# Branch hints and five unread products at the seam between layer 0's front and the joint stage

## The chip, the cores and the metric

The kernel runs on one core of a Trainium2 chip. The metric is the device time of one execution in microseconds (us), lower is better. The profile comes from one further execution of the same program, recorded by the hardware profiler. Names used below: PE is TensorE (PEld its weight loads), DVE is VectorE, ACT is ScalarE, POOL is GpSimd, SP is the engine that issues most transfers. A trailing q (DVEq) means the engine's sequencer: branches, register loads, semaphore work.

## What is computed

The reference is a network of two layers on an image of 64 x 64 pixels with 96 channels. Each layer is a mixer with a residual and then a small MLP with a residual:

```
x = x + conv_ref(ln(x))          # a state-space mixer
t = t + ffn_ref(ln(t))           # t: x as 4096 tokens
```

Layer 0's mixer projects to 192 channels and a gate, applies a 3 x 3 depthwise convolution and silu, and scans the 4096 positions in four directions with 16 states for each channel:

```
log_dA = dt * A;  dB_u = dt * B * u
decay = exp(cumsum(log_dA))
h = decay * cumsum(dB_u / (decay + 1e-12))
y = sum_n(h * C) + u * D_skip
```

The four results are added, normalized, gated and projected back. In layer 0 the decay is so strong that, for inputs like these, only the first positions of each scan direction contribute; the full scan is needed only if the decay is weak. Layer 1's mixer has a full 3 x 3 convolution over channels and a recurrent scan. The MLPs round their operands to 8-bit floats.

## The kernel before, in words

All data of one image stay in on-chip memory as far as possible; the 4096 positions are handled in chunks of 512. The program has these stages in time.

Layer 0's front (`front0`, which calls `scan_ends`) runs from the start to about 102 us. It normalizes, projects and convolves the image, and beside that computes the ends of the four scans, 160 positions each, on small tiles. The order of its instructions is written out: `keep` holds an instruction in program order. The last lines of `scan_ends` (L840 to L867) are, on DVE, the scans of the ends, their product with C and the sums over states (L849, L850); then the smallest decay exponent `low` (L852) and the flag `alive` (L854), which is 1 if the full scan is needed. On PE there are fourteen products of the identity with itself into a bank `warm` that nobody reads (L860), and then two products `yc` (L863) which bring the last part of the ends to both halves of the partitions. `values_load` (L864) loads the flag into a register of each engine. `add_ends` (L875) then adds the ends to the image `y` on DVE, sixteen operations.

The branch is in `layer0` (L317): `with tc.If(self.alive > 0)` holds the full scan `scan_all`. With these inputs the flag is 0, so every engine jumps over the body. In the built program the code of the body lies between the front and what follows (1262 instructions on DVE, 515 on PE, 1201 on ACT, 295 on SP, 221 on POOL). Each engine takes its own branch and, on the path that skips the body, sets semaphores to what the body would have left them at; the stage behind the branch waits for them.

The joint stage (`middle`, L1100 on) does the rest of layer 0 and the front of layer 1 together. It first allocates tiles and issues weight loads on SP and memsets on POOL (`open1`, L1251 to L1287), takes eight banks of PSUM (`slots("bank", ...)`), and issues ten products of the identity with itself into the first bank, which nobody reads (L1129 and L1130). Then a planner takes over: `Order` holds operations with costs, dependencies and leads (`LEAD`), and its `run` writes them out in a fixed order for each engine. The first planned work is `mix0`: means over channels on PE (L1363, L1367), their subtraction on DVE (L1371, L1375), squares on ACT (L1378), the gate on POOL (L1382), variances on PE (L1398).

From about 300 us to the end the scans of layer 1 run (L1998 on DVE, with ACT, POOL, PE and transfers beside), and last layer 1's MLP.

Of the kernel before, what the change touches and what calls it, by code (L numbers as in the profile page):

```python
# [39 lines left out]
P = 128  # L40
# [223 lines left out]
class Net:  # L264
# [37 lines left out]
    def layer0(self, w, w1):  # L302

        tc = self.tc
        self.pools0 = ctx = ExitStack()
        wp = ctx.enter_context(tc.tile_pool(name="mw0", bufs=1))
        yp = ctx.enter_context(tc.tile_pool(name="my0", bufs=1))
        pp = ctx.enter_context(tc.tile_pool(name="pad0", bufs=1))
        self.weights0(wp, w)
        self.y = [yp.tile([P, L // (1 + g)], F32, tag=f"y{g}", name=f"y0{g}") for g in range(2)]  # L310
        pad = self.padded0(pp)
        self.bc_d = [self.scratch(f"bc0{o}", [2, NST, L]) for o in range(2)]
        self.dt_d = [self.scratch(f"dt0{g}", [P, L]) for g in range(2)]
        self.du_d = [self.scratch(f"du0{g}", [P, L]) for g in range(2)]
        self.u_d = [self.scratch(f"u0{g}", [GP[g], L]) for g in range(2)]
        self.front0(wp, w, w1, pad)
        with tc.If(self.alive > 0):  # L317
            self.scan_all()

    def weights0(self, wp, w):  # L320
# [369 lines left out]
    def scan_ends(self, ep, pm, ps, pad, ue, beside):  # L690
# [4 lines left out]
        nc, keep = self.nc, self.keep  # L695
# [12 lines left out]
        o = 0  # L708
# [60 lines left out]
        for i, at in enumerate((XB, XC)):  # L769
            rows = self.dram.tile([4, TS], F32, tag=f"re{i}", name=f"re{i}")  # L770
            t = tile6(f"bce{i}", TS)
            o = 0
# [25 lines left out]
        buckets, o = [], 0  # L798
        for n0, n1, k in BUCKETS:
            buckets.append((n0, n1, n1 - n0, k, slice(o, o + (n1 - n0) * k)))  # L800
            o = buckets[-1][-1].stop
# [42 lines left out]
        for n0, n1, m, k, at in buckets[1:]:  # L844
            add = x[:, :, at]
            if m > 1:
                add = sums[:, :, 0:k]
                states = x[:, :, at].rearrange("p s (n t) -> p s t n", n=m)
                keep(nc.vector.tensor_reduce(add, states, AX.X, ALU.add))  # L849
            keep(nc.vector.tensor_tensor(x[:, :, 0:k], x[:, :, 0:k], add, ALU.add))  # L850
        low = ep.tile([1, 1], F32, tag="low", name="low")
        keep(nc.vector.tensor_reduce(low, t[0:1, 0:P], AX.X, ALU.min))  # L852
        alive = self.cp.tile([1, 1], I32, tag="alive", name="alive")
# [4 lines left out]
        warm = ps.tile([P, CH], F32, tag="e", name="warm")  # L858
# [2 lines left out]
        yc = [pm.tile([P, TE], F32, tag="m", name=f"yc{w}") for w in range(2)]  # L861
        for t, r in zip(yc, LANES):
            keep(nc.tensor.matmul(t, self.dup[r], x[r, 5], start=True, stop=True))  # L863
        self.alive = nc.values_load(  # L864
            alive, min_val=0, max_val=1, skip_runtime_bounds_check_because="the result of a comparison"
        )
# [230 lines left out]
    def keep(self, instruction):  # L1097
        self.tc.keep_in_program_order(instruction)

    def middle(self, w, pool):  # L1100
# [10 lines left out]
        nc, tc = self.nc, self.tc  # L1111
# [12 lines left out]
        def slots(tag, p, n, shape, dtype=F32):  # L1124
            o.slots(tag, [p.tile(shape, dtype, tag=f"{tag}{i}", name=f"{tag}{i}") for i in range(n)])

        pb = banks.enter_context(tc.tile_pool(name="ps_mid", bufs=1, space=PSUM))
        slots("bank", pb, 8, [P, CH])
        for _ in range(10):  # L1129
            self.keep(nc.tensor.matmul(o.free["bank"][0][1][:, 0:P], self.ident, self.ident, start=True, stop=True))  # L1130
        bp = back.enter_context(tc.tile_pool(name="back0", bufs=1))
        for tag, n, shape, dtype in (
            ("r", 2, [P, 2, 4], F32),
# [1443 lines left out]
```

## Time and profile before

| what | us |
|---|---|
| median of three runs (1229.6 to 1230.89) | 1230.8 |
| time of the profiled execution | 1231.9 |
| its span | 1229.9 |
| front's last DVE addition ends (L875) | 102.33 |
| ten unread products begin (L1130) | 105.00 |
| first mean begins (L1363) | 109.34 |
| first subtraction begins (L1371) | 113.22 |
| PE's mean granted clock over the span | 0.877 |

All times below the span are counted from the span's start. Busy time of an engine is time in its data path; waiting and sequencer work are not in it. A product in 32-bit floats takes two passes of PE, so ten products appear as twenty rows. The view of one line lists what ran on each engine and sequencer for that line, with the shortest, median and longest duration in ns and the first and last start. The view of narrow stretches gives busy times of PE, PEld, DVE, ACT and POOL, then the clock that PE was granted (1.00 is full speed), then how busy the transfers were.

### The profile page before, as it was taken

To read this page: it belongs to the slowest core of one execution; us is meant where nothing else is said; L and a number is where in the kernel's file an instruction comes from. 1 tells how busy PE (TensorE), PEld (TensorE's weight loads), DVE (VectorE), ACT (ScalarE), POOL (GpSimd) and SP (SyncE) were. 2 spreads that over 40 slices of the span, in tenths; PEclk is the share of its full clock that TensorE was granted. 3 is DMA by queue.
4 is the path that set the end of the run, shared out by engine and by line. 5 is a ranking of instruction groups with operands and counts; after the bars stand their busy time and mean duration, and the time that the engine had idled before them with its cause. 6 is when DMAs were issued, how large, how long until landed. Compare 5 with 4: busy or idle time off the path is not lost.

```text
span 1229.9 us, 11118 instructions
## 1 busy us (share of the span) xinstructions
PE 1013.7 (82%) x3498; PEld 414.7 (34%) x3498; DVE 1134.9 (92%) x908; ACT 881.8 (72%) x1065; POOL 842.4 (68%) x510
## 2 busy tenths in 40 slices
PE   9997889985278877887787877889778889888986
PEld 5533334321023322222332222233224444343344
DVE  7895787788898999999999999999999999999968
ACT  5682555656568878877888777878878878887626
POOL 3002364352678888888798878987798888886756
PEclk9998989995589887889978788988789999988987
DMA  2252010476763573575734585545736766432201
GB/s 76 67 174 53 1 27 20 124 245 193 235 193 126 182 237 125 172 230 172 239 112 127 194 258 166 180 146 185 233 115 194 246 195 235 142 101 83 103 1 52
DMA packets 79132, 183.14 MB, mean 149 GB/s; under 512 B 21534, under 2 KB 34936, under 8 KB 77688
## 3 DMA queue, kind: packets, MB, share of 16 engines
q1 hardware_dynamic: 78376, 182.16, 47.6%
q8 instruction: 29, 0.48, 0.2%
q14 instruction: 39, 0.32, 0.1%
q10 hardware_dynamic: 688, 0.19, 0.1%
HBM read 159.73 MB, written 21.52 MB: 147 GB/s over the span
## 4 chain that ended last, share of the span: by engine, by line
DVE 46%; issue 11%; PE 10%; ACT 5%; DMA 2%; POOL 1%; SPq 0%; another core or an unknown queue 0%; DVEq 0%; POOLq 0%; ACTq 0%
DVE h1s L1998 14%; DVE xws L1998 13%; DVE h0s L1998 8%; PE hs L2009 4%; DVE x2s L1998 3%; DVE x0s L1998 3%; DVE x1s L1998 3%; PE hs L2013 2%; ACT da L1983 2%; ACT xws L1968 2%; DMA x2s<-bc 1%; PE eo L2123 1%; PE da L2326 1%; POOL hss L2003 1%; DMA kept<-xn 1%
## 5 line engine op out<-in xcount | busy, mean ns | idle before, releaser
L2026 POOL TENSOR_TENSOR kept<-kept,kept 128x1024 f32<-128x1024 f32 x92 | 216.7, 2356 | 82.3 <-issue 40.2
L2003 POOL TENSOR_TENSOR hss<-h1s,xws 128x1024 f32<-128x1024 f32 x96 | 228.0, 2377 | 55.2 <-DVE xws L1998 52.4
L2009 PE MATMUL hs<-h0s,ident 128*128 128x512 f32 x360 | 222.9, 705 | 27.6 <-DVE h0s L1998 24.0
L1983 ACT ACTIVATE da<-dt1s,a 128x1024 f32<-128x1024 f32 x168 | 187.5, 1117 | 71.3 <-DVE xws L1998 55.3
L1998 DVE TENSOR_TENSOR_SCAN xws<-da,xws 128x1024 f32<-128x1024 f32 x96 | 221.6, 2308 | 10.4 <-ACT da L1983 10.3
L1983 ACT ACTIVATE da<-dt0s,a 128x1024 f32<-128x1024 f32 x166 | 185.1, 1115 | 45.1 <-DVE h0s L1998 16.2
L2013 PE MATMUL hs<-hss,ident 128*128 128x512 f32 x368 | 188.1, 603 | 15.4 <-POOL hss L2003 15.3
L1998 DVE TENSOR_TENSOR_SCAN h1s<-da,h1s,xws 128x1024 f32<-128x1024 f32 x72 | 167.3, 2323 | 0.3
L2037 PE MATMUL acc<-kept,fold 128*32 128x512 f32 x368 | 87.6, 687 | 73.8 <-POOL kept L2026 73.8
L2022 ACT COPY kept<-hs 128x512 f32<-128x512 f32 x184 | 107.1, 582 | 47.0 <-PE hs L2013 46.3
L2009 PEld LDWEIGHTS hs<-h0s,ident 128*128 128x128 f32 x360 | 71.5, 216 | 152.4 <-issue 82.3
L2013 PEld LDWEIGHTS hs<-hss,ident 128*128 128x128 f32 x368 | 70.0, 194 | 116.2 <-issue 79.1
L2009 PE MATMUL hs<-x1s,ident 128*128 128x512 f32 x128 | 75.5, 675 | 14.1 <-DVE x1s L1998 14.1
L2009 PE MATMUL hs<-x0s,ident 128*128 128x512 f32 x128 | 73.6, 659 | 14.8 <-DVE x0s L1998 14.8
L1962 POOL TENSOR_TENSOR x1s<-x1s,dus 128x1024 f32<-128x1024 f32 x32 | 75.5, 2361 | 9.0 <-DMA x1s<-bc 9.0
L2009 PE MATMUL hs<-x2s,ident 128*128 128x512 f32 x120 | 69.1, 660 | 14.1 <-DVE x2s L1998 14.1
L1962 POOL TENSOR_TENSOR x2s<-x2s,dus 128x1024 f32<-128x1024 f32 x32 | 75.7, 2364 | 2.7 <-DMA x2s<-bc 2.7
L1998 DVE TENSOR_TENSOR_SCAN x0s<-da,x0s 128x1024 f32<-128x1024 f32 x32 | 73.9, 2310 | 1.1 <-ACT da L1983 1.1
L1998 DVE TENSOR_TENSOR_SCAN x1s<-da,x1s 128x1024 f32<-128x1024 f32 x32 | 73.9, 2308 | 1.1 <-ACT da L1983 1.1
L1998 DVE TENSOR_TENSOR_SCAN x2s<-da,x2s 128x1024 f32<-128x1024 f32 x32 | 73.9, 2311 | 0.6 <-ACT da L1983 0.4
L1968 ACT COPY xws<-x1s 128x1024 f32<-128x1024 f32 x32 | 63.2, 1974 | 5.4 <-POOL hss L2003 5.4
L1968 ACT COPY xws<-x2s 128x1024 f32<-128x1024 f32 x32 | 63.2, 1976 | 4.2 <-POOL x2s L1962 4.2
(374 smaller groups left out, 1887.3 us busy)
## 6 DMA issues: line engine op xcount, KB each, us to landing
kept<-bc SPq DMA_DIRECT2D x92, 512.0 KB
x2s<-bc SPq DMA_DIRECT2D x32, 512.0 KB
x0s<-bc SPq DMA_DIRECT2D x28, 512.0 KB
x1s<-bc SPq DMA_DIRECT2D x28, 512.0 KB
dus<-du SPq DMA_DIRECT2D x20, 512.0 KB
dt1s<-dt SPq DMA_DIRECT2D x20, 512.0 KB
dt0s<-dt SPq DMA_DIRECT2D x20, 512.0 KB
kept<-xn SPq DMA_DIRECT2D x24, 384.0 KB
```

The source lines that it names most:

```text
L1962: keep(nc.gpsimd.tensor_tensor(x, x, du[:, part[j]], ALU.mult))
L1968: keep(copy(grid(xw)[:, w, :], cols(xs[i % 3])[:, w, :]))
L1983: keep(nc.scalar.activation(t, dts[o][:, part[j]], AF.Exp, scale=self.a6[:, g, k : k + 1]))
L1998: keep(nc.vector.tensor_tensor_scan(to, da, x, start, ALU.mult, ALU.add))
L2003: keep(nc.gpsimd.tensor_tensor(cols(hs)[:, w, :], grid(h1)[:, w, :], grid(xw)[:, w, :], ALU.add))
L2009: keep(nc.tensor.matmul(t, self.ident, x[:, chunk(m)], start=k == 0, stop=False))
L2013: keep(nc.tensor.matmul(sums[i, m], self.ident, hs[:, chunk(m)], start=False, stop=True))
L2022: keep(nc.scalar.copy(to, sums.pop((i, j * (SC // CH) + h))))
L2026: keep(nc.gpsimd.tensor_tensor(t, t, times_c_by(i, a), ALU.mult))
L2037: keep(nc.tensor.matmul(to, self.fold4, src, start=k == 0, stop=k == NK - 1))
L2123: keep(nc.tensor.matmul(o[:, j], y[:, j:CH:4], w, start=False, stop=j == 3))
L2326: keep(nc.tensor.matmul(o[:, j], y[r, 2 * k + j : CH : 4], w[r], start=first and j == 0, stop=end and j == 1))
```

## The change

The branch gets the label `full`. In `scan_ends`, between the sums over states and `low`, a hint location for that branch is marked on all five engines, with the hint `LikelyTaken`. Behind `yc`, five products of the identity with itself are added, into the bank `warm`. In `middle` the ten products into the first bank are removed.

```diff
--- before.py
+++ after.py
@@ -314,7 +314,7 @@
         self.du_d = [self.scratch(f"du0{g}", [P, L]) for g in range(2)]
         self.u_d = [self.scratch(f"u0{g}", [GP[g], L]) for g in range(2)]
         self.front0(wp, w, w1, pad)
-        with tc.If(self.alive > 0):
+        with tc.If(self.alive > 0, label="full"):
             self.scan_all()
 
     def weights0(self, wp, w):
@@ -848,6 +848,8 @@
                 states = x[:, :, at].rearrange("p s (n t) -> p s t n", n=m)
                 keep(nc.vector.tensor_reduce(add, states, AX.X, ALU.add))
             keep(nc.vector.tensor_tensor(x[:, :, 0:k], x[:, :, 0:k], add, ALU.add))
+        engines = (nc.vector, nc.scalar, nc.tensor, nc.gpsimd, nc.sync)
+        self.tc.mark_branch_hint_location("full", "LikelyTaken", [e.engine for e in engines])
         low = ep.tile([1, 1], F32, tag="low", name="low")
         keep(nc.vector.tensor_reduce(low, t[0:1, 0:P], AX.X, ALU.min))
         alive = self.cp.tile([1, 1], I32, tag="alive", name="alive")
@@ -861,6 +863,8 @@
         yc = [pm.tile([P, TE], F32, tag="m", name=f"yc{w}") for w in range(2)]
         for t, r in zip(yc, LANES):
             keep(nc.tensor.matmul(t, self.dup[r], x[r, 5], start=True, stop=True))
+        for _ in range(5):
+            keep(nc.tensor.matmul(warm[:, 0:P], self.ident, self.ident, start=True, stop=True))
         self.alive = nc.values_load(
             alive, min_val=0, max_val=1, skip_runtime_bounds_check_because="the result of a comparison"
         )
@@ -1126,8 +1130,6 @@
 
         pb = banks.enter_context(tc.tile_pool(name="ps_mid", bufs=1, space=PSUM))
         slots("bank", pb, 8, [P, CH])
-        for _ in range(10):
-            self.keep(nc.tensor.matmul(o.free["bank"][0][1][:, 0:P], self.ident, self.ident, start=True, stop=True))
         bp = back.enter_context(tc.tile_pool(name="back0", bufs=1))
         for tag, n, shape, dtype in (
             ("r", 2, [P, 2, 4], F32),
```

In the built program two things stand elsewhere than the source suggests. The hint instructions are, on every engine, the first instruction behind the entry branch, at the head of the front. And on DVE `low` stands ahead of the sums over states and `alive` ahead of the last two of the three reductions (L849), rather than behind them and among the additions. The order of the other instructions is the same on all engines.

## The prediction

> **What bounds the kernel now.** I read the page first, its row of busy times.
>
> ```profile
> PE 1013.7 (82%) x3498; PEld 414.7 (34%) x3498; DVE 1134.9 (92%) x908; ACT 881.8 (72%) x1065; POOL 842.4 (68%) x510
> ```
>
> VectorE is busy 92% of the span, most of it with scans (L1998), and the change touches none of them. It can only move when they begin, which is decided at the seam between layer 0's front and the joint stage. So next I read the timeline over that seam (start, duration, engine, line and operation, in brackets the idle time before it and what ended it).
>
> ```profile
> 93.30 3.39 PE L860 MATMUL warm<-ident 128*128 128x128 f32 x28
> ...
> 98.57 0.69 PE L863 MATMUL yc<-bce,dup 64*128 64x160 f32 x4 [1.88 <-issue]
> ...
> 100.83 1.50 DVE L875 TENSOR_TENSOR y<-y,yc 64x64 f32<-64x64 f32 x8
> ...
> 105.00 4.51 PE L1130 MATMUL bank<-ident 128*128 128x128 f32 x20 [5.74 <-DVEq L317]
> ...
> 109.34 2.74 PE L1363 MATMUL bank<-y,mean 128*128 128x512 f32 x6
> ...
> 113.22 1.28 DVE L1371 TENSOR_TENSOR y<-y,bank 128x512 f32<-128x512 f32 x2 [10.89 <-PE bank L1367]
> ```
>
> The front's last work is DVE's adds, done at 102.33 (100.83 + 1.50). TensorE stands idle for 5.74 us until DVE's sequencer is through the branch (L317), then does the ten unread products of L1130, and only at 109.34 starts the first mean (L1363), which somebody reads. Behind it L1371 has waited 10.9 us, and by the view of waits ACT 19.8 and POOL 10.0 us for what follows L1371. So from 102.33 to 113.22 one chain holds everything: branch, ten products, means.
>
> The rows of line 317 show where the branch's time goes (duration in ns, then the start in us).
>
> ```profile
> L317 ACTq COMPARE_BRANCH  x1: 50/50/50, 99.5 to 99.5; - x1
> ...
> L317 PEldq COMPARE_BRANCH  x1: 3737/3737/3737, 99.6 to 99.6; - x1
> L317 DVEq COMPARE_BRANCH  x1: 72/72/72, 101.8 to 101.8; - x1
> L317 ACTq EVENT_SEMAPHORE  x1: 17/17/17, 102.5 to 102.5; - x1
> ...
> L317 PEldq EVENT_SEMAPHORE  x1: 51/51/51, 103.4 to 103.4; - x1
> L317 DVEq EVENT_SEMAPHORE  x1: 21/21/21, 104.8 to 104.8; - x1
> ```
>
> From its branch to the first instruction at the target each engine needs 3.0 us (ACT 99.5 to 102.5, DVE 101.8 to 104.8) or 3.8 us (PE 99.6 to 103.4). DVE branches last: its adds stand ahead of its load of the flag (the row of L864: 545 ns from 101.2). Its 3.0 us are the ones that count; the other four are ready earlier and wait for its event.
>
> Last, the granted clock in narrow stretches (busy times of five engines, then the clock, DMA share, GB/s).
>
> ```profile
> 99.00:99.10 0.10, 0.10 (x3) 0.00 (x0) 0.10 (x1) 0.00 (x0) 0.00 (x0) 0.61 0.00 0
> ...
> 109.20:109.30 0.10, 0.10 (x2) 0.10 (x2) 0.00 (x0) 0.00 (x0) 0.00 (x0) 0.69 1.08 369
> ```
>
> Full before, one half after 99.1, full again from 109.3. So the ten products ran at half clock: 20 passes in 4.34 us, 0.217 each, against 3.39/28 = 0.121 for the same tile at L860.
>
> **The change part by part.**
>
> *Ten products out.* From 105.00 to 109.34 they are alone on the path: 4.34 us.
>
> *Five products in.* They go behind L863 on PE, which ends at 99.26. Ten passes at 0.121 to 0.217 take 1.2 to 2.2 us, so they end by 101.5. What hides them is DVE's adds to 102.33; the cover left is 0.8 us, and without it they would cost at most 2.2. Nobody reads their bank. PE's register load now queues behind them: the sequencer issued L860's 56 entries well ahead of their execution (its wait for L863 is recorded from 94.5, while the last of L860 runs at 96.4), so 20 more entries cost under 1 us and PE's branch moves to at most 100.6. Unhelped by a hint, PE would be through at 104.4, still before DVE. Cost nothing.
>
> *DVE's flag earlier.* In the built program the two tiny operations that make `alive` now stand before the last reductions rather than among the adds (0.27 + 0.13 us, same work). ACT, POOL and SP load it some 4 us sooner, but all three wait for DVE's event, and DVE's own load stays behind its adds. Worth nothing.
>
> *The hints.* In the built program each engine's hint is its first instruction behind the entry branch, some 100 us ahead of the branch it names. Its own cost: ACT's compare-and-branch of 0.05 us is the nearest row; I take 0.05, with ends 0 and 0.5 (a register load), at the span's very start. What it brings no row of this trace shows, so both ends: 0 if it does nothing; at best DVE's 3.0 us vanish, but then the adds' end at 102.33 is next, so the means start at 102.4 instead of 104.96, a gain of 2.55. Below nothing: if it fetched the wrong code, one more fetch of 3.0 to 3.7 us.
>
> Here a rule speaks against the change. The Trainium skill, "Runtime: NRT & Kernel Launch", section "Instruction fetch mechanics", says an engine's instruction memory is refilled in blocks of 256 instructions, two at a time (eight on PE), that prefetch is purely sequential, and that a taken branch out of this window stalls on a fetch. The stall is what the 3.0 us show. Taken strictly, nothing but sequence is prefetched: gain 0. But DVE's front is only 182 instructions in the built program (PE's 426), so by the same page's sizes a target block fetched early need not be displaced before the branch. I take 2.55, because 100 us is ample for a fetch of 3 us and the executed path is the branch's taken one (the row after it stands 3 us later, so its target was not the next code). No run here shows it yet.
>
> *SP's and POOL's first work* (weight loads from 105.05, memsets from 105.13) moves with DVE's event. The first product that needs them (L1305, at 114.03) showed no wait for them, and moves by less than 7 us with them; cost nothing. Without a working hint they stay while PE comes 4.3 us closer; w_in is first in the queue, so still nothing.
>
> *The clock.* The means would start cold. From 109.34 to L1371's start they take 3.88 us at full clock; each microsecond at half clock adds 0.5. The Trainium skill, "TensorE: Matmul & The Clock Gate", section "Part 1: The HAM clock gate", says the gate looks at a free-running window of 3.41 us, lowers the clock after an idle window and raises it after a busy one. The trace agrees: 99.05 to 109.25 is 10.2 us, three windows, with edges at 102.4 and 105.8. By the rule, means that begin at 102.4 run cold to 105.8: 3.4 us, cost 1.7. If yc and the five products (0.2 and 2.2 of the 3.4 us up to 102.4) pass as busy: cost 0. In the worst phase two windows, 6.8 us: cost 3.4. I take 1.7, by this trace's own edges, and because a window with 1.6 us busy (95.6 to 99.05: L860's tail and half of L863) was not enough to hold the clock.
>
> *Sum.* Means start at 102.4 instead of 109.34: 6.94 gained; less 1.7 and 0.05: 5.2. The joint stage's order is fixed per engine and its next waits all hang on L1371, so it moves as a whole and the scans behind it. The profiled execution took 1231.9 (span 1229.9 and 2.0 around it): 1226.7. The median, 1230.8, is 1.1 lower: 1225.6.
>
> **The rivals.**
>
> *The hints do nothing.* For: the rule, and a distance of 100 us. Against: nothing in the trace. The means start at 104.96; the five products end by 101.5, so PE idles 3.4 us and the clock returns at 109.25 as now: 4.3 us cold, cost 2.15. Gain 4.38 - 2.15 = 2.2: 1228.6, from 1226.4 (clock never lost) to 1229.8 (another phase, cost 3.4).
>
> *The gain is lost further on.* The clock drops again in the joint stage (0.89 granted from 140 to 170), and the scans begin behind loads (a 10.7 us wait for x2s in the chain at 315). If those have other causes than the seam, the time stays about 1230.8, within 1.5. Against: these loads follow writes made by the joint stage itself.
>
> *Slower: the hints displace code.* The place is DVE's two-block memory. If a useless block is fetched ahead of the wanted one, the branch costs 3.0 more, and if it has pushed out a block that sequence had brought, another 3.0 comes in the joint stage: 6.0 - 2.2 = 3.8 slower, 1234.6. It decides from more than one extra fetch, since one (3.0 against 2.2) is within 0.8 of no change. Against: the front's 182 instructions leave little to displace.
>
> **How the numbers follow.** A measurement of this kernel can tell about 0.2%, 2.5 us, from no change. Hints work: 0.55, 1225.6, from 1223.9 (no cold cost) to 1227.3 (3.4). Hints idle: 0.27, 1226.4 to 1229.8, in four of ten below 1228.3. Lost further on: 0.11. Slower: 0.07. Faster 0.55 + 0.11 + a little of the third, 0.68; slower 0.07; same 0.25. The range is the first two cases, 1223.8 to 1229.8, 0.82 of the chance.
>
> **What would show it.** No row of L1130; ten passes of the new line between 99.3 and 101.5. DVE's event at L317 within 0.3 us of its branch, or 3.0 behind it: that tells the first case from the second. L1363 at 102.4 or 105.0. L1371 at 107 to 110. The clock's rise between 102.4 and 109. The shift of L1371 against the shift of the first scan at 299.65 (L1832) tells the loss further on. Wrong would be: another gap of 3 us on DVE or PE, or any start of a scan that does not move with L1371.

## The result and the profile after

The changed kernel took 1226.42 us, the median of 22 runs (1220.7 to 1232.76), beside 1230.44 for the kernel before in the same rounds (22 runs, 1227.05 to 1236.62). The ratio is 0.9963, with a 95% interval from 0.9951 to 0.9976: 3.0 to 6.0 us faster, 4.5 in the middle. The profiled execution took 1224.26 us, with a span of 1222.4; that is 7.5 us of span less than before, more than the ratio says. Most of the experiments below are about this difference.

The page's row of busy times of the kernel after:

```profile
PE 1009.6 (83%) x3488; PEld 411.8 (34%) x3488; DVE 1134.6 (93%) x908; ACT 882.0 (72%) x1065; POOL 843.4 (69%) x510
```

Ten passes of PE fewer (3488 against 3498) and otherwise the same work; DVE's busy time is unchanged to 0.3 us. The time came from a stretch in which DVE waited.

The timeline over the seam, kernel after (start, duration, engine, line, operation, idle time before). The added lines shift the numbers: L862 was L860, L865 was L863, L879 was L875 (the five products of L867 are new), and in the joint stage L1365 was L1363 and L1373 was L1371.

```profile
92.39 3.39 PE L862 MATMUL warm<-ident 128*128 128x128 f32 x28
...
98.31 0.99 PE L865 MATMUL yc<-bce,dup 64*128 64x160 f32 x4 [2.52 <-issue]
...
99.24 2.50 PE L867 MATMUL warm<-ident 128*128 128x128 f32 x10
100.51 1.50 DVE L879 TENSOR_TENSOR y<-y,yc 64x64 f32<-64x64 f32 x8
...
102.27 2.81 PE L1365 MATMUL bank<-y,mean 128*128 128x512 f32 x6 [0.54 <-DVEq L317]
...
106.23 1.28 DVE L1373 TENSOR_TENSOR y<-y,bank 128x512 f32<-128x512 f32 x2 [4.22 <-PE bank L1369]
```

The first mean starts at 102.27, 0.26 us behind the end of DVE's adds (100.51 + 1.50 = 102.01); before it was 7.0 us behind them (109.34 against 102.33). PE's idle time at the branch shrank from 5.74 to 0.54 us, no row stands between it and the means, and L1373 waits 4.2 us instead of 10.9.

The rows of line 317, kernel after (duration in ns, then the start in us):

```profile
L317 ACTq COMPARE_BRANCH  x1: 68/68/68, 94.5 to 94.5; - x1
...
L317 ACTq EVENT_SEMAPHORE  x1: 17/17/17, 95.0 to 95.0; - x1
...
L317 PEldq COMPARE_BRANCH  x1: 397/397/397, 99.1 to 99.1; - x1
L317 DVEq COMPARE_BRANCH  x1: 84/84/84, 101.5 to 101.5; - x1
L317 PEldq EVENT_SEMAPHORE  x1: 51/51/51, 101.8 to 101.8; - x1
L317 DVEq EVENT_SEMAPHORE  x1: 21/21/21, 102.1 to 102.1; - x1
```

DVE's way from the branch to the first instruction behind it takes 0.6 us where it took 3.0, ACT's 0.5 for 3.0, and PE's branch itself 397 ns for 3737. The event at 102.1 and the end of the adds at 102.0 now lie within 0.1 us of each other, so less of the branch would hardly start the means earlier. ACT, POOL and SP branch 5 us earlier, and it gains nothing, since POOL then waits 83.2 us for DVE's event (it was 85.6).

The granted clock, kernel after, in narrow stretches (stretch, its length, busy times of five engines, clock, DMA share, GB/s):

```profile
98.40:98.50 0.10, 0.10 (x2) 0.10 (x3) 0.10 (x1) 0.00 (x0) 0.00 (x0) 0.61 0.00 0
98.50:99.00 0.50, 0.50 (x4) 0.40 (x3) 0.50 (x3) 0.00 (x0) 0.00 (x0) 0.50 0.00 0
...
101.80:101.90 0.10, 0.00 (x0) 0.00 (x0) 0.10 (x2) 0.00 (x0) 0.00 (x0) 0.82 0.00 0
101.90:102.50 0.60, 0.23 (x1) 0.26 (x2) 0.11 (x2) 0.00 (x0) 0.09 (x1) 1.00 0.00 0
```

It falls at 98.42, so yc and the five products ran at half speed (2.50 us for ten passes), and it is back at 101.83, one window of 3.41 us later and ahead of the first mean. In this execution the means ran warm.

The shift does not get lost behind the seam. L1373 starts 6.99 us earlier than before (106.23 against 113.22), the scan that the prediction calls the first, now L1834, 6.97 (292.68 against 299.65; it is the second of its line, the first starts 2.4 us ahead of it), the last scan of the kernel 7.6 (1166.84 against 1174.42), and the span ends 7.5 earlier.

### The profile page after: what moved, and what is told of

Read it like the earlier page. It is cut to its first block, busy times and chain, and to the rows that moved or that the text cites. A ratio compares the mean times of both kernels' runs of the same rounds, so it can differ in the third digit from the quotient of the medians.

```text
span 1222.4 us, 11103 instructions
## 1 busy us (share of the span) xinstructions
PE 1009.6 (83%) x3488; PEld 411.8 (34%) x3488; DVE 1134.6 (93%) x908; ACT 882.0 (72%) x1065; POOL 843.4 (69%) x510
## 4 chain that ended last, share of the span: by engine, by line
DVE 42%; PE 14%; issue 10%; ACT 5%; DMA 3%; POOL 1%; another core or an unknown queue 0%; DVEq 0%; SPq 0%; POOLq 0%; ACTq 0%
DVE h1s L2000 13%; DVE xws L2000 12%; DVE h0s L2000 8%; PE hs L2011 7%; PE hs L2015 3%; DVE x2s L2000 3%; DVE x0s L2000 3%; DVE x1s L2000 2%; ACT da L1985 2%; DMA kept<-xn 2%; ACT xws L1970 2%; DMA dt<-hss 1%; PE acc L2039 1%; PE da L2328 1%; POOL hss L2005 1%
## 5 line engine op out<-in xcount | busy, mean ns | idle before, releaser
L1964 POOL TENSOR_TENSOR x0s<-x0s,dus 128x1024 f32<-128x1024 f32 x28 | 66.3, 2367 | 0.0
```

The source lines that it names most:

```text
L1964: keep(nc.gpsimd.tensor_tensor(x, x, du[:, part[j]], ALU.mult))
```

## The experiments

**The theory**: each half of the change takes its own piece off one chain. The hints take most of DVE's way from its branch to the next instruction (2.4 us), the ten products' place gives 4.3, and what the means lose by starting cold depends on where the clock's windows happen to fall. **The rivals**: the hints do nothing and the ten products were all of it; the five products, not the hints, bring the gain, by keeping the clock; or the seam's gain is noise of the clock elsewhere in the kernel. Ratios are against the kernel before on the same chip; its median was 1231.7 us for the first four kernels, 1231.81 for the next four and 1230.84 for the last four.

### The hints alone

```diff
-        for _ in range(5):
-            keep(nc.tensor.matmul(warm[:, 0:P], self.ident, self.ident, start=True, stop=True))
...
+        for _ in range(10):
+            self.keep(nc.tensor.matmul(o.free["bank"][0][1][:, 0:P], self.ident, self.ident, start=True, stop=True))
```

> The kernel after, with the ten products back in the joint stage and the five behind yc taken out: the hints alone. My theory: DVE's event at line 317 comes within 0.7 us of its branch, as in the kernel after (101.5 to 102.1), the ten products begin at 102.3 instead of 105.0, and everything behind moves by 2.6 us: about 0.2% faster, ratio 0.998. The ten products still run at half clock, 4.3 us, unless the clock's window happens to help. Rival (the short branch comes from something else in the change): the ten products begin at 105.0 and the time is that of before.

Measured: 1231.06 us (14 runs), ratio 0.9995 [0.9977, 1.0013]. Its timeline and its rows of L317:

```profile
102.41 4.61 PE L1132 MATMUL bank<-ident 128*128 128x128 f32 x20 [3.33 <-DVEq L317]
...
110.86 1.28 DVE L1373 TENSOR_TENSOR y<-y,bank 128x512 f32<-128x512 f32 x2 [8.72 <-PE bank L1369]
```

```profile
L317 DVEq COMPARE_BRANCH  x1: 84/84/84, 101.6 to 101.6; - x1
L317 DVEq EVENT_SEMAPHORE  x1: 21/21/21, 102.2 to 102.2; - x1
```

The ten products start at 102.41 instead of 105.00 and the first subtraction at 110.86 instead of 113.22: 2.4 us, as the step on the hints has it. The timing neither confirms nor excludes it: 2.4 of 1231 would be the expected ratio of 0.998, and the interval holds both that and 1.

### The products alone

```diff
-        engines = (nc.vector, nc.scalar, nc.tensor, nc.gpsimd, nc.sync)
-        self.tc.mark_branch_hint_location("full", "LikelyTaken", [e.engine for e in engines])
```

> The kernel before, with the ten products taken out of the joint stage and five put behind yc, without any hint. My theory: DVE's event stays 3.0 us behind its branch, the first mean begins at 105.0 instead of 109.3, and the means run cold for some of their 3.9 us, at a cost of 0 to 3.4 us: first subtraction at 109 to 112, gain 1.0 to 4.4, most likely 2.2, ratio 0.998. Rival (hints and products are the same gain seen twice, since in both the seam ends at a common point): gain as large as the whole change, 0.9963. Rival (clock stays low): no gain.

Measured: 1228.91 us (22 runs), ratio 0.9977 [0.9963, 0.999]: 1.2 to 4.6 us faster. Its timeline:

```profile
98.87 1.38 PE L865 MATMUL warm<-ident 128*128 128x128 f32 x10
...
104.70 4.45 PE L1363 MATMUL bank<-y,mean 128*128 128x512 f32 x6 [4.46 <-DVEq L317]
...
110.30 1.28 DVE L1371 TENSOR_TENSOR y<-y,bank 128x512 f32<-128x512 f32 x2 [8.21 <-PE bank L1367]
```

Without hints DVE's 2.9 us are back (branch at 101.6, event at 104.5; PE's branch 3420 ns) and PE stands idle for 4.46 us. The first subtraction gains 2.9 us: the ten products' 4.3, less means that ran cold (5.60 us from the first mean to the subtraction, 3.96 in the kernel after), and a front that ends 0.2 us earlier. This is near the 2.2 of the prediction's first rival. In the traces it is not what the whole change does; the timing alone does not separate the two, since this interval reaches 0.9963, the whole change's ratio.

### The hints without the five products

```diff
-        for _ in range(5):
-            keep(nc.tensor.matmul(warm[:, 0:P], self.ident, self.ident, start=True, stop=True))
```

> The kernel after, with the five products taken out and nothing in their place: hints, no warming. My theory: the first mean begins at 102.3 as in the kernel after, but at half clock for 3.4 to 6.8 us, and its first subtraction comes 1.7 to 3.4 us later than the 106.2 of the kernel after, at 108 to 109.6: ratio about 0.998. Rival (the five products do nothing, the clock's return is a matter of where its window lies): first subtraction and time as in the kernel after, 0.996.

Measured: 1229.51 us (22 runs), ratio 0.9975 [0.9959, 0.9991]. The first mean starts at 102.49, cold, and the subtraction follows at 107.89, 5.40 us later. The subtraction is 1.66 us later than in the kernel after, 1.44 of it between mean and subtraction, by the clock. But it is one execution: in a second profile of the kernel after (below) the same stretch took 5.74 us with the five products in place. The timing lies on the side of a gain by them (0.9975 against 0.9963), but the intervals overlap.

### The clock held through the seam

More unread products in the same two places, so that PE has no long idle stretch between 92 and 101.

```diff
-        for _ in range(14):
+        for _ in range(22):
...
-        for _ in range(5):
+        for _ in range(9):
```

> The kernel after, with twenty-two products in place of fourteen ahead of yc and nine in place of five behind it, so that PE has almost no gap from 92 to 101.4. My theory: the clock never falls in whichever place its window lies, the means begin at 102.3 and run at full clock, the first subtraction comes at 106.2 in every run: up to 1.7 us better than the kernel after in the mean of runs, ratio about 0.995. Rival (the spread of the times has another cause than the clock at this seam): same as the kernel after, 0.9963. If the clock falls all the same, the nine products take 3.9 us, end at 103 and cost 0.8 us.

Measured: 1223.15 us (6 runs, 1222.28 to 1224.11), ratio 0.9927 [0.9901, 0.9953]. The clock stays at 1.00 from 92 to 146 us. The first mean starts at 102.43 and the subtraction at 106.39: warm, as in the kernel after, and not earlier. Even nine products (2.27 us, ending at 101.28) are hidden by DVE's adds, which end at 102.17. In its one profile it gains nothing over the kernel after, and yet it is faster in the runs. That fits a clock term that the kernel after pays in some executions and this one in none. The next kernels test this.

### The same kernel once more

The kernel after, unchanged.

> The kernel after, unchanged, once more. In the six profiles so far every rise and fall of PE's clock lies on a grid of 3.413 us whose offset differs from execution to execution. My theory: so this profile differs from that of the kernel after only by its offset; the first mean begins at 102.3 again, the first subtraction at 106.2 to 107.9, and what differs else differs in the tail behind the last scan, which took 52.7 to 59.8 us so far. Its ratio is within 0.9951 to 0.9976 again. Rival (the seam itself varies by other things): the first mean begins elsewhere than 102.1 to 102.6.

Measured: 1227.11 us (22 runs), ratio 0.9962 [0.9946, 0.9978], the same result as the first time. Its profile is another:

```profile
98.89 0.63 PE L865 MATMUL yc<-bce,dup 64*128 64x160 f32 x4 [2.53 <-issue]
...
102.86 4.59 PE L1365 MATMUL bank<-y,mean 128*128 128x512 f32 x6 [1.02 <-DVEq L317]
...
108.60 1.28 DVE L1373 TENSOR_TENSOR y<-y,bank 128x512 f32<-128x512 f32 x2 [6.00 <-PE bank L1369]
```

The means ran cold (4.59 us for the group that took 2.81), and the subtraction stands at 108.60, 2.4 us later than in the first profile. Of these, 1.8 are clock; the other 0.6 stand already ahead of yc (98.89 against 98.31). The first mean at 102.86 is outside what was expected for it by 0.3 us for that reason, and the subtraction by 0.7: the length of the front varies too, and not the clock alone.

Why the same instructions run warm once and cold once shows in the edges of the clock. In each of the 14 profiles of this study every fall and rise of it lies on a grid of 3.41 us, and the grid's position to the span's start differs from execution to execution. Whether it moves at an edge has to do with how busy PE was in the window before it. Three such windows, of three executions, with the clock at 0.50 in each. The kernel after, first profile (the columns as above; the first busy time is PE's):

```profile
98.42:101.83 3.41, 3.32 (x14) 2.69 (x14) 3.24 (x15) 0.00 (x0) 0.00 (x0) 0.50 0.02 5
```

The kernel after, second profile:

```profile
99.57:102.98 3.41, 2.38 (x11) 2.12 (x11) 2.86 (x14) 0.00 (x0) 0.00 (x0) 0.51 0.02 5
```

The kernel of the next experiment (the seam is the same in it):

```profile
98.68:102.09 3.41, 3.03 (x14) 2.40 (x12) 3.24 (x16) 0.00 (x0) 0.00 (x0) 0.50 0.02 5
```

Behind the first the clock rose; behind the second and third it did not. With 3.12 of 3.41 us busy (98.90 to 102.31 in the profile with DVE's hint alone, below) it rose too. Yet in the profile with the hints on all engines but DVE, where the seam's products are the same, it did not rise behind a window with the same 3.12 us:

```profile
98.19:101.60 3.41, 3.12 (x14) 2.82 (x14) 3.27 (x16) 0.00 (x0) 0.00 (x0) 0.50 0.05 12
101.60:105.01 3.41, 0.48 (x3) 0.22 (x3) 0.64 (x4) 0.00 (x0) 0.03 (x1) 0.50 0.01 5
```

So the five products and yc bring the clock back in some positions of the grid and not in others, and nearly a full window of them is no guarantee. In one more execution the means were warm because the clock had not fallen at all. It is the kernel after with six products added in the tail (its second profile, below), and there an edge of the grid cuts PE's idle stretch ahead of yc in two:

```profile
93.64:97.06 3.42, 2.02 (x19) 1.83 (x17) 3.32 (x6) 0.00 (x0) 0.00 (x0) 1.00 0.02 7
97.06:100.47 3.41, 1.94 (x14) 1.61 (x14) 3.19 (x11) 0.00 (x0) 0.00 (x0) 1.00 0.03 7
```

Over all windows of the 14 profiles only half of a limit shows. No window with less than 1.45 us of PE busy kept a full clock, and none with less than 2.71 us raised a lowered one; but windows that were busy throughout lie on both sides, so the busy time that a profile shows isn't what decides alone.

### Six unread products in the tail

The runs of one kernel scatter by 10 us and more, which is more than the seam can give. The timelines showed one place: from the start of the last scan to the end of the span the profiles of the first round took 52.7, 55.5, 55.6 (twice), 59.7 and 59.8 us for one and the same work. PE waits 1.9 us there, behind the last scan. The timeline of the kernel with the hints alone (52.7 us), and that of the kernel with the products alone (59.7 us):

```profile
1176.43 1.48 PE L2289 MATMUL acc<-x2s,fold 128*32 128x512 f32 x4 [1.95 <-DVE kept L2359]
1177.84 4.05 PE L2328 MATMUL da<-x0s,kept 64*128 64x192 f32 x16
```

```profile
1173.73 2.35 PE L2287 MATMUL acc<-x2s,fold 128*32 128x512 f32 x4 [1.93 <-DVE kept L2357]
1176.01 5.51 PE L2326 MATMUL da<-x0s,kept 64*128 64x192 f32 x16
```

The same products, warm in the one and cold in the other. In the second the clock fell at 1173.0, in that wait, and stayed at one half to 1203.7. Its windows, one line for each step of the grid (PE's busy time first, the clock third from the end):

```profile
1169.60:1173.00 3.40, 2.20 (x14) 1.12 (x13) 3.40 (x4) 0.00 (x0) 1.59 (x2) 0.99 0.00 0
1173.00:1176.40 3.40, 2.67 (x5) 0.75 (x6) 0.87 (x2) 0.00 (x0) 3.40 (x3) 0.50 0.02 7
1176.40:1179.80 3.40, 3.40 (x12) 3.40 (x12) 1.21 (x3) 0.00 (x0) 3.40 (x3) 0.50 0.00 0
1179.80:1183.20 3.40, 3.40 (x12) 1.62 (x12) 2.39 (x8) 0.35 (x2) 1.39 (x2) 0.50 0.00 0
...
1200.30:1203.70 3.40, 3.40 (x25) 2.33 (x23) 3.04 (x8) 2.89 (x7) 2.54 (x5) 0.50 0.00 0
1203.70:1212.00 8.30, 6.37 (x59) 4.66 (x58) 7.69 (x19) 6.67 (x16) 7.32 (x10) 1.00 0.08 26
```

In the half-clock windows shown PE is busy for 2.67 to 3.40 of 3.40 us, and the clock does not come back. The edit puts six products that nobody reads into the wait, inside the helper that does the fold and ahead of its fourth call's own products.

```diff
+        folds = iter(range(7))
...
+            for _ in range(6 if next(folds) == 3 else 0):
+                keep(nc.tensor.matmul(unread[:, 0:HID], self.identb[0:CD], w1, start=True, stop=True))
```

In the kernel after:

> The kernel after, with six unread products in PE's 1.9 us wait behind the last scan (ahead of the fourth fold of the tail). My theory: the spread of the times comes from the clock falling in that wait in some offsets of the grid: with the products it does not fall there, the tail takes 53 to 54 us in every run, the times spread by less than 6 us rather than 12, and the median gains about 2 us on the kernel after: ratio 0.994. Rival (the spread has another cause): median and spread as in the kernel after, 0.9963.

Measured: 1224.23 us (6 runs), ratio 0.9932 [0.9907, 0.9957], tail 52.2 us.

In the kernel before:

> The kernel before with the six unread products in the tail's wait (ahead of the fourth fold) and nothing else. My theory: the tail behind the last scan takes 52 to 54 us in every offset of the clock's grid instead of 52.7 to 59.8, the median gains 2 to 4 us: ratio 0.997 to 0.998. Set beside the kernel after with the same six products it leaves the seam alone to differ. Rival (the tail gains only in the kernel after): ratio 1.000.

Measured: 1229.18 us (13 runs), ratio 0.9982 [0.9964, 1.0001], tail 52.25 us. The gain of 1.7 us by the medians is less than the 2 to 4 that were expected, and the interval reaches 1: by the timing it is not resolved.

And again in the kernel after, beside it on the same chip:

> The kernel after with the six products in the tail, once more, on the same chip as the kernel before with them. My theory: it is 5 us faster than that one (the seam's 7.0 less a cold cost of 1.7 to 2.4 in most offsets and none in a few): ratio to before 0.993, 0.004 below that of the kernel before with the six. Rival (the change's gain is the 4 us of the medians and the tail adds to it by accident): difference between the two of 3 us or less, or of 7.

Measured: 1222.77 us (6 runs), ratio 0.9932 [0.991, 0.9954], tail 52.3 us. In its timeline the products lie in the wait, and the fold behind them is warm:

```profile
1170.34 1.15 PE L2290 MATMUL unread<-w,identb 96*128 96x384 bf16 x6
1172.35 1.48 PE L2293 MATMUL acc<-x2s,fold 128*32 128x512 f32 x4 [0.87 <-DVE kept L2363]
```

With the tail's clock held in both, the change is worth 1229.18 - 1222.77 = 6.4 us by the medians and 0.9982 - 0.9932 = 0.0050, or 6.2 us, by the ratios. The two intervals leave some 3.5 us either way, so this does not contradict the 4.5 us of the plain pair; it excludes that the tail made the gain. In the three profiles with these products the tail takes 52.2 to 52.3 us, and 52.8 in a fourth below. Their runs still scatter by 6.5, 7.4 and 6.3 us, where less than 6 was expected: the tail is a part of the scatter and not all of it.

### Which engine's hint it is

One profiled run each, for the seam's rows and not for the time.

```diff
-        engines = (nc.vector, nc.scalar, nc.tensor, nc.gpsimd, nc.sync)
+        engines = (nc.vector,)
```

> The kernel after with the hint on DVE alone. My theory: DVE's event comes 0.6 us behind its branch at 101.5; PE needs its 3.4 to 3.8 us again from 99.1 to about 102.9, so PE becomes the last and the first mean begins at about 102.9 instead of 102.3; ACT, POOL and SP take 3 us from 94.5 and are ready by 98, so their hints are worth nothing: seam 0.6 us later than in the kernel after. Rival (the other engines' hints carry part of the gain): first mean later than 103.5.

```profile
L317 PEldq COMPARE_BRANCH  x1: 3400/3400/3400, 99.5 to 99.5; - x1
L317 DVEq COMPARE_BRANCH  x1: 84/84/84, 101.9 to 101.9; - x1
L317 DVEq EVENT_SEMAPHORE  x1: 21/21/21, 102.5 to 102.5; - x1
L317 PEldq EVENT_SEMAPHORE  x1: 51/51/51, 102.9 to 102.9; - x1
```

These are the rows of L317 with the hint on DVE alone. DVE is through at 102.5, and now PE's own way through the branch without a hint, to 102.9, ends last: the first mean starts at 103.18, and the wait before it names PE's sequencer in place of DVE's. PE's hint is therefore worth about 0.5 us here, and those of the other three nothing.

```diff
-        engines = (nc.vector, nc.scalar, nc.tensor, nc.gpsimd, nc.sync)
+        engines = (nc.scalar, nc.tensor, nc.gpsimd, nc.sync)
```

> The kernel after with hints on ACT, PE, POOL and SP, but none on DVE. My theory: DVE's event stays 3.0 us behind its branch, at 104.6, and the first mean begins at 104.7 to 105.0 as without any hint: the four other hints gain nothing at all. Rival (some other engine's branch is what the seam waits for): first mean before 104.

With the hints on all but DVE its branch is at 101.8 and its event at 104.7, 2.9 us as before, and the first mean starts at 104.84:

```profile
104.84 4.60 PE L1365 MATMUL bank<-y,mean 128*128 128x512 f32 x6 [2.93 <-DVEq L317]
```

Four hints without DVE's bring the start of the means nothing. In this build DVE makes the flag late again (ACT's branch is at 99.4, not 94.5), so the flag's earlier place belongs to DVE's hint. It makes no difference to the path.

### The held clock in the seam and in the tail

The kernel with 22 and 9 products again, and with the six in the tail added.

> The kernel with twenty-two and nine products at the seam, once more. My theory: the first subtraction comes at 106.2 to 106.6 in every offset of the grid, 1.7 us earlier in the mean than in the kernel after; the narrow spread of its first six runs (1222.3 to 1224.1) was chance, since its tail is that of the kernel after; median 1225 with a spread of 7 us or more, ratio 0.995. Rival (the seam decides the tail too): ratio 0.993 with a spread of 2 us again.

Measured: 1224.36 us (6 runs, 1222.95 to 1230.24), ratio 0.9946 [0.9926, 0.9965]. The first subtraction is at 106.91 and the seam warm, but the tail of its profile is 59.7 us. The 106.91 is 0.3 us outside what was expected; its front ends 0.5 us later than in the first profile (102.69 against 102.17). The narrow spread of the first six runs did not come again, and how much more it gives than the plain change is not resolved (0.9927 and 0.9946, against 0.9963 and 0.9962).

> Both together: twenty-two and nine products at the seam and six in the tail. My theory: seam at 106.2 to 106.6 and tail at 52 to 54 us in every offset: ratio 0.991 to 0.992, the fastest of all, with a spread below 4 us. Rival (they share one cause and don't add): ratio as in either alone, 0.993.

Measured: 1221.67 us (6 runs), ratio 0.9928 [0.9907, 0.9949]; its profile has the shortest span of all, 1219.3 us, with the subtraction at 106.27 and a tail of 52.8. It beats the kernel before by 6 to 11 us. Against the six tail products alone it is not resolved: 0.991 to 0.992 and a spread below 4 us were expected, 0.9928 and 5.6 us came out, and the tail products alone have 0.9932 on the same chip. Whether the two gains add stays open.

## Why the prediction was right, step by step

The forecast was 1225.6 us and the median came to 1226.42. The whole interval is clear of no change (at least 0.24% faster).

Several executions of each kernel show the sum better than one. In us from the span's start, the plain kernels and those with the six tail products, which leave everything ahead of the tail as it is ("first scan" is the prediction's, the second of its line):

| profile | first mean | mean to subtraction | first subtraction | first scan | last scan |
|---|---|---|---|---|---|
| before | 109.34 | 3.88 | 113.22 | 299.65 | 1174.42 |
| before, tail products | 109.75 | 3.89 | 113.64 | 300.02 | 1174.45 |
| after | 102.27 | 3.96 | 106.23 | 292.68 | 1166.84 |
| after, again | 102.86 | 5.74 | 108.60 | 296.20 | 1171.39 |
| after, tail products | 102.38 | 5.50 | 107.88 | 295.50 | 1170.36 |
| after, tail products again | 102.14 | 3.96 | 106.10 | 293.63 | 1168.69 |

- **The start of the means.** Forecast 6.94 us earlier; the means of the rows above give 109.55 - 102.41 = 7.1. Both terms hold: the branch (2.4 us in the profile of the hints alone, for 2.55) and the ten products' place (4.3). DVE's event follows its branch by 0.6 us rather than within 0.3. That costs nothing, because the branch at 101.5 overlaps with the last adds, which end at 102.0. The hints' own cost, put at 0.05 us, cannot be told: the front's end varies by more from execution to execution (102.0 and 102.6 in two of the kernel after).
- **The rule of sequential prefetch** (the Trainium skill, "Runtime: NRT & Kernel Launch", section "Instruction fetch mechanics"). Where it said that nothing would be gained, the runs decide against it: 3.0 us become 0.6 on DVE with the hint and stay 2.9 without it, in a kernel that differs otherwise only in the place of the flag. What the rule calls a stall is there; that nothing but sequence is fetched does not fit what DVE, PE and ACT do with this hint. The traces show the shorter way and not the fetch itself.
- **The five products at no cost.** Right, but closer than said. The clock had fallen, so they took 2.50 us, where at most 2.2 was forecast, and ended at 101.74, 0.27 us ahead of the adds' end and not 0.8. Nine cost nothing either, in three profiles that kept them at full clock. PE's register load moved from 99.0 to 98.5, not back, so its branch is at 99.1 instead of the feared 100.6.
- **The clock.** This is the term that was mis-sized. The forecast took 1.7 us; the four executions of the kernel after show 0, 1.8, 1.5 and 0, 0.8 in the mean. The two ends that were named, no cost and a whole window cold, both occur. Of the two executions without cost, one had the clock raised by the products, as the prediction had it; in the other the clock never fell. What failed is the choice of one edge: it used the position of the grid in the profile before, and at the seam that position differs in each execution. That is also why the profiled execution moved by 7.5 and not by 5.2, and why L1373 at 106.2 is ahead of the 107 to 110 and the clock's rise at 101.8 ahead of the 102.4 to 109 that were named.
- **Carried through.** The first profile carries all of it (6.99 at the subtraction, 6.97 at the first scan). In the mean of the rows above, 6.2 us at the subtraction are 5.3 at the first scan and 5.1 at the last. The 0.9 go in three of the four executions, in the stretch between 145 and 300 us, where their clock differs as well (0.67, 0.65 and 0.61 from 260 to 280 us, 0.73 in the first profile). One place can be seen: in these three, ACT's L1713 at 276 to 279 us waits 3.12 us for PE's products of L1694, in the first profile 1.32. It does not explain all, since the profile with the hints alone has the same wait and takes only 0.2 us more than the kernel before over this stretch. So the rival "lost further on" has a small part of the truth; the clock is the likely cause, and not tested.
- **SP, POOL and the flag** are as said: POOL's first memset moved from 105.13 to 102.41 with DVE's event, and the products that need SP's first load showed no wait for it.
- **The slower case**: no new gap of 3 us appeared on DVE or PE at the seam, and the first scan moved by as much as the subtraction. No sign that anything was displaced.

The nearness of 1225.6 to 1226.42 is partly luck of cancelling parts: the clock in the seam cost 0.9 us less than forecast, and 1.1 us went behind it. What stays open: the timing alone does not show the 2.4 us of the hints (ratio 0.9995, from 0.9977 to 1.0013), which rest on the traces; that the hints bring DVE's code ahead of its branch is argued from the shorter way; and the worth of the five products by themselves, 0.9975 without them against 0.9963 with them, is inside the intervals.

## What to carry to other kernels

At a seam where every engine branches, find the engine whose sequencer comes last and price its own way from the branch to its first instruction; help for the others is worth only what they would be late next (0.5 us of PE here, nothing of three). Products that only keep the clock belong into a wait that something else ends, and are sized so that no window is mostly idle wherever its edges fall: with 22 and 9 products the emptiest window at the seam had 2.27 us of PE busy, and the clock held in all three profiles. Before a few microseconds of a 1200 us kernel are read from a trace, take several profiles of the same kernel and compare milestone by milestone, since one execution shows one position of the clock's grid.

## What the runs showed beyond that

- The position of the clock's grid moves the whole kernel by more than this change does: a wait of 1.9 us behind the last scan left the tail at 52.7, 55.5 or 59.7 us, 7 us out of 1230, for the same instructions. Differences of 0.15 to 0.2 us in that position go with different tails. In the ten profiles without the tail products, the step of the grid in that wait lies 2.74 us behind the start of the last scan (one profile; the clock stays up, 52.7 us), 2.89 to 3.00 us (five; it is down for 30.7 us, tail 59.7 to 59.8) or 3.21 to 3.43 us (four; down for 10.2 us, 55.5 to 55.6).
- With six small products in the wait the clock fell in none of four profiles (52.2 to 52.8 us). Only one of these, at 3.13 us, lies between positions at which it fell without them; the other three, at 3.50 to 3.56 us, have no counterpart. So the traces support that the products hold the clock there, and one position carries the comparison.
- A clock that has fallen can stay down although PE is busy throughout: in the profile of the products alone from 1176.4 to 1186.6, three windows. At the seam one window with 3.12 of 3.41 us was enough in one profile and not in another. What tells them apart I did not test; the matmuls of the tail use 64 rows or 32 columns of the array, or a narrow type, and so does yc (64 rows), while the seam's unread products use all 128 by 128.
- POOL is the one engine that the hint did not help: 2.7 us from its branch to its first instruction in the kernel after (94.5 to 97.2), 3.0 in another profile with the hint (99.5 to 102.5), 3.4 in the kernel before (99.5 to 102.9) and 2.6 with the hint on DVE alone (94.9 to 97.5). Nothing waited for it here.
